# Residual rows behind their chunk's tokens, and five tiles in one routing chain, in the last stage of a graph and mixture-of-experts kernel

## Chip, core and metric

The program runs on one core of one Trainium2 chip. The metric is the device time of one execution in microseconds (us). Six runs of the kernel before gave a median of 3677.98 us, from 3671.99 to 3696.28.

## What is computed

The reference is four rounds, each a graph layer and then a feed-forward layer with experts, over x of 3125 rows (nodes) by 256. Both edits lie in the last layer, which in the reference is this:

```python
mu = mean(x, -1); var = mean(square(x - mu), -1)
xn = (x - mu) * rsqrt(var + EPS) * gamma + beta     # a second layer norm: x is already normed
logits = xn @ Wr + br                               # 8 experts
top_vals, top_idx = top_k(logits, 2); w = softmax(top_vals)
for e in range(8):
    h = gelu(xn @ W1[e] + b1[e])                    # 256 -> 512
    y = y + (h @ W2[e] + b2[e]) * w_full[..., e]    # 512 -> 256
x = x + y
```

## The kernel before

**Tiles and chunks.** The 3125 rows lie in 25 tiles of 128, with partition p of tile t holding row 128 t + p. The tile `XX` keeps x and its normed form beside each other. The last layer works through three chunks of tiles, `CH3` (L97): chunk 0 is tiles 0 to 4, with 208 places for each expert (2 blocks of 104); chunks 1 and 2 are tiles 5 to 14 and 15 to 24, with 384 places (3 blocks of 128).

**Routing, `route3` (L2624) and `Experts.route` (L1989).** One chain routes a group of up to five tiles. For each tile, ScalarE applies the batch norm of the graph layer (L2632), TensorE turns it back to rows (L2638) and VectorE adds it to x (L2640). Then come the statistics (L1891, L1892), two inverse square roots in small VectorE steps over the whole group (L221 to L232, twice, because of `twice=True`), the normed rows (L1911 on ScalarE or L1913 on VectorE), and for each tile a transpose (L1866), a scaled copy (L1873 or L1876) and the logits (L1928, L1930). The top two are found for the whole group in small VectorE steps (L289 to L317, with a Tanh on ScalarE, L307). Two matmuls count the places (L2013, L2014), more small steps make the positions (L2019 to L2057), and GpSimd scatters each tile's rows twice, once for each of its two experts, into the chunk's table `xg` in HBM (L2070, issued by the helper in L160). A memset of one element (`apart`, L1940) stands ahead of each scatter.

**Residual rows, `base_rows` (L2232).** Each tile of x is also scattered to the output (L2241, issued in L160 as `out_x<-XX,idI`), 25 scatters in all. The experts' results are added onto these rows later.

**Experts, `run` (L2132).** For each chunk and each of the 8 experts: SyncE loads the expert's places (L2107) and its weights (L2127, two halves, two buffers each); TensorE turns the places (L2155) and ScalarE scales them (L2160); TensorE makes the hidden layer (L2093), with a Gelu on ScalarE (L2181), and the output (L2097); VectorE adds the bias (L2204), ScalarE or VectorE multiplies by the routing weight (L2210, L2212), and GpSimd adds the rows onto the output in HBM, one indirect DMA for each block (L2247): 2 for each expert of chunk 0 and 3 in the others, 64 in all. An expert's adds wait until those of the expert before it in the same chunk have landed, and the first expert's wait for the chunk's residual rows (`add_rows`, L2251). The result `ro_y` has two buffers.

**What sets the order.** The engines work in program order, and a small planner (`Plan`, L1791) writes that order down. Each chain yields an engine, a planned duration and what it needs; the planner always takes the step that can start first, and among those within 0.05 us the one of the lowest rank. Routing chains are added with ranks 0, 1, 2 and so on (L2659), tokens, weights and residual rows with rank 0, experts with 1.5. Two routing chains are under way at a time: chain i + 2 starts when chain i has placed its scatters.

**Two runs of the planner.** The first, `pl.run(routed, ...)` (L2664), ends when every group is routed and no buffer of a ring is open. Then `rest` (L2258) asks whether any expert had more rows than places: a matmul turns the flag (L2262), VectorE reduces it (L2266), each engine loads it to a register and branches (L2268). What was not placed before is placed behind the branch by the second `pl.run()` (L2667).

The groups of the routing chains are (chunk, first tile, tiles):

```python
groups3 = ((0, 0, 3), (0, 3, 2), (1, 5, 5), (1, 10, 5), (2, 15, 5), (2, 20, 5))
```

Below, the five-tile groups at tiles 5, 10, 15 and 20 are called B, C, D and E; the two small groups of chunk 0 are a and b, and the group of tiles 0 to 4 is A. The experts are e0 to e7 of chunk 0, 1 or 2.

Of the kernel before, what the change touches and what calls it, by code (L numbers as in the profile page):

```python
# [115 lines left out]
def tile_gnn_ffn(ctx: ExitStack, tc: tile.TileContext, a: dict, out: bass.AP):  # L116
# [7 lines left out]
    @contextmanager  # L124
    def psums(**bufs):
        with tc.tile_pool(name="psum", bufs=1, space=PSUM) as p:
            before = dict(banks)
            banks["pool"], banks["bufs"] = p, bufs
            yield
            banks.update(before)  # L130

    def ps(tag, shape):
        return banks["pool"].tile(shape, F32, name=tag, tag=tag, bufs=banks["bufs"][tag])
# [11 lines left out]
    def bcast(src, n, pool, name):  # L145

        t = pool.tile([P, n], F32, name=name)
        nc.sync.dma_start(t, bass.AP(tensor=src.tensor, offset=src.offset, ap=[[0, P], [1, n]]))
        return t
# [9 lines left out]
    def put(table, idx, src):  # L159
        return nc.gpsimd.indirect_dma_start(  # L160
            out=table, out_offset=bass.IndirectOffsetOnAxis(ap=idx, axis=0), in_=src, in_offset=None)
# [106 lines left out]
    def load_w(pool, w, name):  # L268

        k, n = w.shape  # L270
        t = pool.tile([P, k // P, n], F32, name=name)
        nc.sync.dma_start(t, w.rearrange("(k p) n -> p k n", p=P))
        return t
# [1609 lines left out]
    def norm_steps(dst, src, n, pool, pre, ready, twice=False, which=("ACT",)):  # L1883


        st = pool.tile([P, GT, 6], F32, name=pre + "st", bufs=1)
        mv = pool.tile([P, GT, 2], F32, name=pre + "mv", bufs=1)
        nm = pool.tile([P, GT], F32, name=pre + "nm", bufs=1)
        for i in range(n):
            f = yield "DVE", 0.41, (ready[i],)  # L1890
            nc.vector.bn_stats(st[:, i, :], src[:, i, :])  # L1891
            nc.vector.bn_aggr(mv[:, i, :], st[:, i, :])  # L1892
        s = {}
        f = yield from small_steps(rsq_steps(s, "r", mv[:, :n, 1], n, pool, pre, 1), f)
        r = s["r"]
        if twice:
            v2 = pool.tile([P, GT], F32, name=pre + "v2", bufs=1)
            f = yield "DVE", 0.26, (f,)
            nc.vector.tensor_mul(v2[:, :n], mv[:, :n, 1], r)
            nc.vector.tensor_mul(v2[:, :n], v2[:, :n], r)  # L1900
            f = yield from small_steps(rsq_steps(s, "r", v2[:, :n], n, pool, pre + "2", 1), f)
            f = yield "DVE", 0.08, (f,)
            nc.vector.tensor_mul(s["r"], s["r"], r)
            r = s["r"]
        f = yield "DVE", 0.08, (f,)
        stt(nm[:, :n], mv[:, :n, 0], -1.0, r, op0=OP.mult, op1=OP.mult)
        done = []
        for i in range(n):
            done.append((yield which, 0.58, (f,)))
            if plan[0].on == "ACT":  # L1910
                nc.scalar.activation(dst[:, i, :], src[:, i, :], AF.Identity, bias=nm[:, i : i + 1], scale=r[:, i : i + 1])  # L1911
            else:
                nc.vector.tensor_scalar(dst[:, i, :], src[:, i, :], r[:, i : i + 1], nm[:, i : i + 1], op0=OP.mult, op1=OP.add)  # L1913
        return done

    def logit_steps(lg, src, g, w, b, n, ready, R, pool, name, us, *args, **kw):

        last = None
        for i in range(g + 1):
            if i < g:  # L1920
                xt = pool.tile([P, 2, P], F32, name=name, bufs=2)
                xf = yield from turned_steps(R["tp"], xt, src[:, i, :], ready[i], us, *args, **kw)
            if i:
                f = yield "PE", 0.4, (last[1], R["u"])
                free = R["u"].take()
                pl_ = ps("u", [P, 2, D])[:, 0, :n]
                for k in range(2):
                    nc.tensor.matmul(pl_, last[0][:, k, :], w[:, k, :], start=(k == 0), stop=(k == 1))  # L1928
                f = yield "DVE", 0.08, (f + slack[0],)
                nc.vector.tensor_add(lg[:, i - 1, :], pl_, b)  # L1930
                free.t = f
            last = (xt, xf)
        return f
# [3 lines left out]
    def apart():  # L1937


        nc.gpsimd.memset(gap, 0.0)  # L1940

    class Experts:
# [289 lines left out]
        def base_rows(self):  # L2232

            for c, (t0, t1, _, _) in enumerate(self.chunks):
                for t in range(t0, t1):
                    while self.x_in[t].t is None:
                        yield None, 0.0, (self.x_in[t],)
                    h = NV if t == NT - 1 else P
                    f = yield "POOL", 1.4, (self.x_in[t],)
                    apart()  # L2240
                    st = put(self.table, idI[:h, t : t + 1], X[:h, t, :])  # L2241
                    self.in_order(st, [])
                    self.bases[c].append(st.ins)
                    self.based[c].add(f)
# [296 lines left out]
    with tc.tile_pool(name="w3", bufs=1) as wp:  # L2541
# [3 lines left out]
        def halves(name, k):  # L2545
            t = wp.tile([P, 2], F32, name=name)
            nc.sync.dma_start(t, a[k].rearrange("(k p) -> p k", p=P))
            return t
# [64 lines left out]
        with tc.tile_pool(name="f3", bufs=1) as fp, psums(tp=2, mm=2, y=2, u=2):  # L2613
            g3, b3 = halves("f_ga", "L3_ffn_gamma"), halves("f_be", "L3_ffn_beta")
            rw = load_w(fp, a["L3_ffn_Wr"], "f_rw")
            br = bcast(a["L3_ffn_br"], 8, fp, "f_br")
            ex3 = Experts("L3_ffn", 8, AF.Gelu, CH3, fp, xg3, None, g3, b3, out)

            pl = plan[0] = Plan()
            R = {"tp": Ring(2), "mm": Ring(2), "y": Ring(2), "u": Ring(2)}  # L2620
            groups3 = ((0, 0, 3), (0, 3, 2), (1, 5, 5), (1, 10, 5), (2, 15, 5), (2, 20, 5))
            routed, befores = All(len(groups3)), [At(0.0), At(0.0)]

            def route3(c, t0, g, pre, before, after):  # L2624
                yield None, 0.0, (before,)
                s = slice(t0, t0 + g)
                ready = []
                for t in range(t0, t0 + g):
                    yn = fp.tile([P, 2, P], F32, name=pre + "yn", bufs=2)
                    f = yield "ACT", 0.85, ()  # L2630
                    for k in range(2):
                        nc.scalar.activation(yn[:, k, :], Y[:, k, t * P : (t + 1) * P], AF.Identity,  # L2632
                                             bias=be[:, k : k + 1], scale=ga[:, k : k + 1])
                    f = yield "PE", 0.3, (f, R["u"])
                    free = R["u"].take()
                    pt = ps("u", [P, 2, D])[:, 0, :]
                    for k in range(2):
                        nc.tensor.transpose(pt[:, k * P : (k + 1) * P], yn[:, k, :], ident)  # L2638
                    f = yield "DVE", 0.33, (f,)
                    nc.vector.tensor_add(X[:, t, :], X[:, t, :], pt)  # L2640
                    free.t = ex3.x_in[t].t = f
                    ready.append(f)
                ready = yield from norm_steps(XN[:, s, :], X[:, s, :], g, fp, pre + "n", ready, twice=True,
                                              which=("ACT", "DVE"))
                lg = fp.tile([P, GT, 8], F32, name=pre + "lg")
                f = yield from logit_steps(lg[:, :g], XN[:, s, :], g, rw, br, 8, ready, R, fp, pre + "xt", 0.42, g3, b3,
                                           which=("ACT", "DVE"))
                yield from ex3.route(c, t0, g, lg[:, :g], f, X, R, pre)
                after.t = f
                routed.add(f)  # L2650

            def experts3():
                for c in range(3):
                    yield from ex3.run(c, R)

            with tc.manual_schedule(engines={EN.PE, EN.DVE, EN.Activation, EN.Pool, EN.SP}):
                for i, q in enumerate(groups3):
                    befores.append(At())
                    pl.add(i, route3(*q, f"f{i % 2}_", befores[i], befores[i + 2]))  # L2659
                pl.add(0, ex3.tokens())  # L2660
                pl.add(0, ex3.weights())
                pl.add(0, ex3.base_rows())
                pl.add(1.5, experts3())
                pl.run(routed, R.values())  # L2664
                ex3.rest(range(NT))
                pl.meet(6.0)
                pl.run()  # L2667
# [64 lines left out]
```

## Time and profile before

| what | value |
|---|---|
| median of the six runs | 3677.98 us |
| profiled execution | 3683.83 us |
| its span (what the views cover) | 3682.1 us |
| TensorE, share of the span busy | 61% |
| VectorE, GpSimd, ScalarE | 46%, 46%, 26% |
| granted TensorE clock, mean | 0.763 |

All times of the trace are from the start of the span. "PE" is TensorE's matmul row and "PEld" its weight load, DVE is VectorE, ACT ScalarE, POOL GpSimd, SP SyncE. A line of a timeline has the start, the duration, the engine, the line of the kernel, the instruction, output <- inputs, shapes and the count of instructions merged into it; in brackets stands how long the engine was idle before and what ended that. TensorE does a float32 matmul in two instructions, so counts in the trace are twice those in the code. The table of windows has for each stretch the busy time of every engine with its instructions in parentheses, then the granted clock (1.00 is full), the DMA engines' mean busy share and GB/s.

The last layer's routing begins at about 3312 us, and the span ends at 3682.1; the edits can reach only these 370 us.

### The profile page before, as it was taken

What the parts mean: (1) busy time and instruction counts of PE and PEld (TensorE: products, weight loads), DVE (VectorE), ACT (ScalarE), POOL (GpSimd) and SP (SyncE); (2) the same over time, 40 slices, a digit from 0 to 9 for tenths busy, and PEclk for the clock granted to TensorE, in tenths of its full rate; (3) what the DMA queues carried; (4) which work ended last, traced back from release to release, by engine and by line L of the source; (5) the groups of instructions that cost most, each with busy time, mean ns of one, the idle gap of its engine ahead of it and who ended that gap; (6) DMA issues with size and microseconds to landing.
All of it is one profiled execution on the core that took longest, in us unless ns stands there. A gap on an engine that the chain in (4) does not pass through costs nothing. (4 is left out here: it accounts for less than half of the span.)

```text
span 3682.1 us, 35829 instructions
## 1 busy us (share of the span) xinstructions
PE 2243.0 (61%) x10124; PEld 1535.4 (42%) x10124; DVE 1684.8 (46%) x6003; ACT 941.8 (26%) x2072; POOL 1694.5 (46%) x1976
## 2 busy tenths in 40 slices
PE   6999667688887796692213664566621021225798
PEld 2444334355554475572102453455510021124676
DVE  3554335555657675333555345246743143336511
ACT  3555232233333342220001221122300000013333
POOL 2200254354545510415665454444457576654744
PEclk8999778689988898795555785778855555555899
DMA  8999776467776530604322563556423233323665
GB/s 293 366 373 352 240 234 190 123 219 226 245 222 180 169 97 34 251 35 156 86 82 83 172 197 113 161 177 212 154 75 106 80 96 89 90 91 102 163 156 119
DMA packets 244620, 608.06 MB, mean 165 GB/s; under 512 B 47342, under 2 KB 111439, under 8 KB 231466
## 3 DMA queue, kind: packets, MB, share of 16 engines
q1 hardware_dynamic: 138346, 321.21, 26.3%
q0 software_dynamic: 103824, 282.18, 25.4%
q10 hardware_dynamic: 2224, 2.11, 0.2%
q8 instruction: 87, 1.43, 0.2%
q14 instruction: 139, 1.14, 0.1%
HBM read 395.45 MB, written 211.44 MB: 165 GB/s over the span
## 5 line engine op out<-in xcount | busy, mean ns | idle before, releaser
L156 POOL DMA_INDIRECT g<-part,e_code x392 | 375.3, 958 | 593.7 <-DMA f<-in_attr 199.0
L156 POOL DMA_INDIRECT g_rows<-tab,srcI x413 | 401.0, 971 | 274.5 <-DVE ACC L2461 117.5
L156 POOL DMA_INDIRECT g_row<-tab,srcI x413 | 396.2, 959 | 193.6 <-issue 111.8
L646 PE MATMUL t<-w_big,n_xt 128*128 128x512 f32 x800 | 359.0, 605 | 21.0 <-issue 8.7
L2093 PE MATMUL mm<-ro_xt,ro_w 128*128 128x192 f32 (+3 forms) x928 | 253.4, 428 | 74.1 <-issue 40.6
L2097 PE MATMUL y<-ro_w,ro_h 128*96 128x256 f32 (+2 forms) x1040 | 259.3, 405 | 43.5 <-issue 26.1
L2595 PE MATMUL mm<-g_xt,c_wr 128*128 128x128 f32 x200 | 48.9, 389 | 367.0 <-issue 296.0
L2585 DVE TENSOR_TENSOR ACC<-ACC,g_row 128x256 f32<-128x256 f32 x413 | 174.0, 424 | 177.0 <-DMA g_row<-tab,srcI 147.5
L2093 PEld LDWEIGHTS mm<-ro_xt,ro_w 128*128 128x128 f32 x928 | 188.3, 224 | 124.3 <-issue 58.0
L646 PEld LDWEIGHTS t<-w_big,n_xt 128*128 128x128 f32 x800 | 151.8, 194 | 206.6 <-issue 184.4
L1011 PE MATMUL w<-xt,w_big 128*128 128x256 f32 (+1 forms) x832 | 227.9, 406 | 8.2 <-issue 8.2
L2097 PEld LDWEIGHTS y<-ro_w,ro_h 128*96 128x96 f32 (+2 forms) x1040 | 189.3, 188 | 94.5 <-issue 30.3
L883 DVE TENSOR_TENSOR g<-pw,g 128x512 f32<-128x512 f32 x196 | 127.8, 687 | 198.0 <-remote 51.4
L2461 DVE SCALAR_TENSOR_TENSOR ACC<-g_rows,g_e,ACC 128x256 f32<-128x256 f32 x413 | 201.1, 487 | 25.6 <-DVE ACC L2461 5.9
L1020 PE MATMUL w<-w_big,b_h 128*128 128x256 f32 x800 | 209.6, 399 | 2.8 <-issue 2.8
L892 PE MATMUL agg<-g,s 128*32 128x256 f32 x1568 | 155.2, 450 | 76.1 <-ACT p_out L896 27.9
L2595 PEld LDWEIGHTS mm<-g_xt,c_wr 128*128 128x128 f32 x200 | 40.5, 282 | 374.8 <-issue 299.6
L1011 PEld LDWEIGHTS w<-xt,w_big 128*128 128x128 f32 x832 | 154.2, 204 | 65.9 <-issue 45.9
L1020 PEld LDWEIGHTS w<-w_big,b_h 128*128 128x128 f32 x800 | 153.7, 199 | 41.0 <-issue 16.7
L649 ACT COPY n_tst<-t 128x512 f32<-128x512 f32 x200 | 116.8, 585 | 198.8 <-PE t L646 179.0
L2181 ACT ACTIVATE ro_h<-mm,ro_w 128x192 f32<-128x192 f32 (+3 forms) x232 | 107.1, 464 | 228.4 <-PE mm L2093 109.1
L160 POOL DMA_INDIRECT xg<-XX,ro_pos x100 | 100.6, 1006 | 140.6 <-issue 78.9
(593 smaller groups left out, 4186.1 us busy)
## 6 DMA issues: line engine op xcount, KB each, us to landing
part<-n_tst SPq DMA_DIRECT2D x100, 1024.0 KB
ro_w<-in_L_ffn_blocks SPq DMA_DIRECT2D x58, 514.0 KB
ro_w<-in_L_ffn_blocks SPq DMA_DIRECT2D x58, 512.0 KB
part<-p_out SPq DMA_DIRECT2D x98, 256.0 KB
xg<-zero SPq DMA_DIRECT2D x78, 200.0 KB
f<-in_attr SPq DMA_DIRECT2D x49, 256.0 KB
b_at<-in_edge_attr SPq DMA_DIRECT2D x50, 224.0 KB
tabn<-v SPq DMA_DIRECT2D x11, 768.0 KB
```

What stands on the lines that cost most here:

```text
L156: return nc.gpsimd.indirect_dma_start(out=dst, out_offset=None, in_=table, in_offset=bass.IndirectOffsetOnAxis(ap=idx, axis=0))
L646: nc.tensor.matmul(pt.rearrange("p r d -> p (r d)"), xt_of[t][:, k, :], wrel[:, k, 2 * i : 2 * i + 2, :].rearrange("p r d -> p (r d)"), st ...
L649: nc.scalar.copy(stage[0][:, o : o + 2, 0, :], pt)
L883: nc.vector.tensor_tensor(m, biased.pop(0), m, op=OP.mult)
L892: nc.tensor.matmul(pa[32 * j : 32 * j + 32, h, :], s[:, 2 * j + h, :], rows[4 * g + 2 * (j // 2) + h][:, j % 2, i * D : (i + 1) * D], star ...
L1011: nc.tensor.matmul(ph, w["01"][:, e, k, i * P : (i + 1) * P], xt[:, k, : n * h], start=(k == 0), stop=(k == 1))
L1020: nc.tensor.matmul(py, last[:, k, i * h : (i + 1) * h], w["02"][:, e - 1, k, :], start=(k == 0), stop=(k == 1))
L2093: nc.tensor.matmul(ph, w[:, o : o + P], xt[:, k, :], start=(k == 0), stop=(k == 1))
L2097: nc.tensor.matmul(py, h[:, i, s], w[:, i * D : (i + 1) * D], start=(i == 0), stop=(i == self.fc - 1))
L2181: nc.scalar.activation(h[:, i, :], ph, self.act, bias=w1[:, j : j + 1])
L2461: stt(u, g[:, r, :D], e[:, r0 + r : r0 + r + 1], u, op0=OP.mult, op1=OP.add)
L2585: nc.vector.tensor_tensor(u, u, rows.pop(r), op=OP.max)
```

## The change

1. `base_rows` now waits until all token scatters of the chunk have been placed (`self.sent[c]`), before it places the chunk's residual rows. The rows are the same and go to the same places.
2. Tiles 0 to 4 are routed in one chain of five instead of a chain of three and a chain of two. There are five chains rather than six.

```diff
         def base_rows(self):
             for c, (t0, t1, _, _) in enumerate(self.chunks):
+                while self.sent[c].t is None:
+                    yield None, 0.0, (self.sent[c],)
                 for t in range(t0, t1):
-                    while self.x_in[t].t is None:
-                        yield None, 0.0, (self.x_in[t],)
                     h = NV if t == NT - 1 else P
-                    f = yield "POOL", 1.4, (self.x_in[t],)
+                    f = yield "POOL", 1.4, (self.x_in[t], self.sent[c])
                     apart()
                     st = put(self.table, idI[:h, t : t + 1], X[:h, t, :])
...
-            groups3 = ((0, 0, 3), (0, 3, 2), (1, 5, 5), (1, 10, 5), (2, 15, 5), (2, 20, 5))
+            groups3 = ((0, 0, 5), (1, 5, 5), (1, 10, 5), (2, 15, 5), (2, 20, 5))
```

Because a planner writes the order, the two edits move much more than they name. In the changed program's order of instructions:

- **GpSimd.** Before: 5 residual rows, 7 token scatters of chunk 0, 5 residual rows of chunk 1, the last 3 of chunk 0, and so on; ahead of the branch lie 50 token scatters, all 25 residual rows and all 16 adds of chunk 0. After: 10 token scatters of chunk 0, 2 of chunk 1, the 5 residual rows of chunk 0, 8 of chunk 1, adds of e0, 7 of chunk 1, adds of e1, 3 of chunk 1, the 10 residual rows of chunk 1, adds of e2, and then token scatters of chunk 2 and adds of e3 to e6 in turn. The 10 residual rows of chunk 2 and the 2 adds of e7 come behind the branch, ahead of the adds of chunk 1.
- **TensorE.** Before: ranks of a and b, L2638 of B, logits of B, L2638 of C, ranks of B, then e0 of chunk 0; then the logits of C, e1, the rest of D's L2638, e2, logits of D among e3's matmuls, e4, logits of E among e5's, ranks of E, e6, e7, the transposes and half the hidden layer of e0 of chunk 1, the branch. After: L2638 of A and B (ten tiles in turn), logits and ranks of A and B, L2638 of C, logits of C, then e0 with C's ranks behind its hidden layer; L2638 of D, e1, logits of D among e2's matmuls, L2638 of E and D's ranks, e3, logits of E (three of them ahead of e4's first matmul), e4, ranks of E, e5, e6, e7, the branch. Nothing of chunk 1 is ahead of the branch.
- **VectorE** issues 68 fewer instructions: the small steps of one chain. Nine tiles of L2640 stand ahead of the first statistics (four before), and B's statistics alternate with the first small steps of A. `apart` and every other helper are unchanged.

## The prediction

> **What bounds the kernel now.** The edits reach only the last 370 us, so I read the windows by stage first, then TensorE's and GpSimd's timelines at the joints, and the chain of waits last. Windows:
>
> ```profile
> 3308.00:3343.00 35.00, 13.75 (x52) 9.96 (x52) 26.23 (x192) 11.53 (x28) 6.02 (x11) 0.51 0.28 110
> 3343.00:3374.00 31.00, 12.47 (x50) 9.30 (x51) 19.78 (x90) 8.87 (x21) 20.69 (x39) 0.50 0.29 97
> 3374.00:3492.00 118.00, 96.49 (x427) 80.45 (x426) 62.48 (x345) 47.97 (x111) 80.21 (x129) 0.80 0.58 157
> 3492.00:3507.00 15.00, 9.70 (x38) 7.34 (x39) 1.56 (x6) 3.08 (x6) 4.50 (x6) 0.89 0.39 100
> 3507.00:3682.00 175.00, 164.93 (x686) 122.53 (x684) 27.83 (x74) 66.28 (x119) 80.72 (x95) 0.99 0.58 139
> ```
>
> The columns are PE, PEld, DVE, ACT, POOL, clock, DMA share, GB/s. There are three regimes: a front of small VectorE steps (3308 to 3374), chunk 0's experts with routing among them (to 3492), and, behind the branch, chunks 1 and 2, where TensorE is busy 94% at full clock.
>
> The chain of waits names GpSimd's adds (L2247) and their DMAs for the tail, which would make the residual rows matter there. The timelines say otherwise; first all engines, then GpSimd alone:
>
> ```profile
> 3535.00 5.34 PE L2097 MATMUL y<-ro_w,ro_h 128*128 128x256 f32 x24
> 3539.43 0.51 ACT L2210 ACTIVATE ro_y<-ro_y,ro_wt 128x256 f32<-128x256 f32 x1 [3.18 <-issue]
> 3540.18 5.32 PE L2093 MATMUL mm<-ro_xt,ro_w 128*128 128x384 f32 x16
> 3540.22 1.57 POOL L2247 DMA_INDIRECT out_x<-ro_y,ro_at  x1 [5.56 <-ACT ro_y L2210]
> ```
>
> ```profile
> 3495.21 1.58 POOL L160 DMA_INDIRECT xg<-XX,ro_pos  x1 [0.20 <-issue]
> 3502.91 0.10 POOL L1940 MEMSET gap<- 128x1 f32 x1 [6.12 <-DMA xg<-XX,ro_pos]
> 3507.23 1.59 POOL L2247 DMA_INDIRECT out_x<-ro_y,ro_at  x1 [4.22 <-ACT ro_y L2210]
> ```
>
> GpSimd sits idle 5.56 us before each expert's first add, for ScalarE, which waits for TensorE; TensorE's hidden layers start 11.0 us apart (3529.19, 3540.18) with no gap. So the tail is TensorE's, and the end moves with the time at which TensorE gets through chunk 0 and the branch. TensorE in chunk 0:
>
> ```profile
> 3374.14 0.93 PE L2155 MATMUL tp<-ident,ro_x 104*128 104x104 f32 x4
> 3375.34 5.68 PE L2093 MATMUL mm<-ro_xt,ro_w 128*128 128x208 f32 x16 [0.27 <-ACT ro_xt L2160]
> ...
> 3384.68 0.60 PE L1866 MATMUL tp<-ident,XX 128*128 128x128 f32 x4
> ...
> 3392.32 1.04 PE L1928 MATMUL u<-f_rw,f_xt 128*128 128x8 f32 x4 [2.73 <-ACT f_xt L1873]
> ...
> 3394.39 1.73 PE L2093 MATMUL mm<-ro_xt,ro_w 128*128 128x208 f32 x4
> ...
> 3409.54 3.98 PE L2093 MATMUL mm<-ro_xt,ro_w 128*128 128x208 f32 x16
> ...
> 3470.35 5.89 PE L2093 MATMUL mm<-ro_xt,ro_w 128*128 128x208 f32 x16
> ```
>
> Here the logits of C stand between e0 and e1 from 3384.68 to 3394.39 and half idle, and the same 16 instructions take 3.98 us in e2 but 5.68 in e0 and 5.89 in e6.
>
> **The change, by TensorE's path.** Sums are made against the profiled execution (3683.83 us: span 3682.1 and 1.7 around it), 5.85 above the median of 3677.98; I take the difference over to the median.
>
> 1. *Start of e0: +3.3.* Nine tiles of L2640 now stand ahead of the first statistics, not four; in the trace they come 0.77 us apart (3313.49, 3314.27, 3315.04): +3.9. Five pairs of B's statistics (0.53 each) alternate with A's first small steps, which otherwise go 0.2 apart with both chains in the gaps: 5 x 0.43 = +2.2. Five tiles instead of three wait for one top-two pass, with B's copies between: +1.0. B's places then follow A's, as long as E's took alone from its ranks (3470.1) to its first scatter (3474.27): +4.2. So C's first L2640 goes from C standing behind B (B's own was at 3342.7) to 3342.7 + 11.3 = 3354.0. From there to a last logit a five-tile group took 3342.7 to 3366.0, 23.3 us, giving 3377.3; e0's transposes stand right behind, against 3374.14. Tokens are no bound: A's first scatter at about 3350, ten at 1.27 us, 3363 (before: 3361.0), landed and loaded well before 3377. In the 23.3 lies a stall of 4 to 5 us of VectorE and ScalarE at 3358.4 that the trace doesn't explain; without it the term is -0.7. The other end: if A and B go one behind the other, B's 30.6 us alone (3342.7 to its ranks at 3373.3) end at 3373.3, and e0 starts 23.3 later at 3396.6: +22.5. I take +3.3, the row with both chains' steps in each other's gaps being what the trace shows at 3319 to 3324.
> 2. *C's logits leave chunk 0: -10.4*, the 9.7 us from 3384.68 to 3394.39 and 0.7 for the fifth logit among e1's matmuls. They are now in the front, inside the 23.3 above.
> 3. *Clock: -3.9.* e1 ran cold after the stalls of C's logits (5.8 us for its 16 instructions against 3.8 in e2, without overlaps); after the change it stands where e2 stood, behind an expert's work without a long wait: -2.0. E's ranks held TensorE 2.44 us and left e6 cold (5.7 against 3.8): -1.9. The other end is 0 for both.
> 4. *E's ranks and logits: -1.0.* The ranks come after 8 us of e4's work instead of 6, so the wait of 2.44 goes; three logits ahead of e4's matmuls wait for copies: C's waited 1.36 and 2.73 in that position, B's not at all; I take +1.4. Ends -2.4 and +1.7.
> 5. *Half of e0 of chunk 1 moves behind the branch: 0.* It took 3486.72 to 3491.51, 4.8 us; behind the branch the same transposes, the wait for the copy (1.28) and 8 instructions. The branch itself keeps its price (3491.78 to 3497.30). VectorE's bias of e7 now stands ahead of the check: +0.4.
> 6. *GpSimd: 0.* Of the five rows of chunk 0 nothing is won: at 3314 to 3321 GpSimd had nothing else. Chunk 1's ten rows, 12.7 us, delay e2's adds by some 5 us and chunk 2's tokens, which nobody needs before 3590. Chunk 2's ten and e7's two adds (10 x 1.27 + 2 x 1.9 = 16.5) come behind the branch. GpSimd comes back 5.6 us after TensorE (3502.91, 3497.30) and is free for chunk 1 at 22.1 after it; e0's rows are ready at about 14. So it starts 8 late. Cover: each expert leaves it over 5 us idle, and both buffers of `ro_y` allow TensorE 11 us of lead. If the wait for landings took all idle time, the lateness would stay: +8. But at the chunks' last experts the adds began 10.35 us after the previous ones (3573.21, 3583.56), so 0.65 each is regained at least, 9.8 over 15 experts. SyncE's order of tokens and weights is the same but for three loads moved by one place at the branch; each is needed 10 us or more after it.
>
> Sum: 3.3 - 10.4 - 3.9 - 1.0 + 0.4 = **-11.6 us**: 3672.2 in a profile, 3666.4 as a median.
>
> [...]
>
> **Rivals.**
>
> - *A front as long as the gain.* The change is meant to send tokens first, but by term 1 tokens go out later (3363 against 3361), because ten tiles share one round. If B's copies also block A's on VectorE and ScalarE by another 10 us, e0 starts 13.3 late, and 13.3 - 14.9 = -1.6 is left: 3676. For it: VectorE was already busy 75% at 3308 to 3343 with five tiles. Against: the small steps of two chains fit in each other's latency.
> - *All of TensorE's gaps close.* Without C, chunk 0 has only D and E among its experts; if e1 to e7 run warm (8 x 7.8 us as e2 with its output, and 1.9 for a cold e0), ten tiles of D and E take 1.5 each in L2638, L1866 and L1928 (2.0 in the groups, mostly at half clock) and their waits stay at 10, it takes 89.3 us, not 112.8 (3374.1 to 3486.9): -23.5 + 3.3 + 0.4 = -19.8: 3658. For it: e7 ran so. Against: D's and E's waits for VectorE (3.0 and 2.8) left the clock at half afterwards.
> - *GpSimd's late start stays in the tail.* Its 8 us come back at the end: -4: 3674. Against it the 10.35 above.
> - *Slower: A and B in sequence.* VectorE works in program order; if one instruction of B that waits for TensorE stands ahead of A's chain round after round, C starts after B. e0 at 3396.6: +22.5 - 10.4 - 3.9 - 1.0 + 0.4 = +7.6: 3686. It decides from e0 starting later than 3374.1 + 14.9 = 3389.
>
> **How the numbers follow.** Forecast 0.60 (3666.4, own range 3659 to 3674), long front 0.15, closed gaps 0.13, late GpSimd 0.05, slower 0.07. The range takes in closed gaps and reaches near the slower case, as the runs of before themselves spread 24 us: 3655 to 3684. A difference under 0.5% (18.4 us) is about what measurement can't tell from no change: faster than 3659.6 is the closed gaps and an edge of the forecast, 0.16; slower than 3696.4 needs e0 33 us late, 0.04; within, 0.80.
>
> **What would show it.** In the profile after: e0's transposes at about 3377, with C's logits just before; A's first token scatter near 3350; e1's 16 instructions in about 4 us; TensorE at the branch near 3480 and back near 3486; ten residual rows right after it on GpSimd, idle time before adds back to about 5 us within a few experts; hidden layers still 11.0 us apart. Wrong if e0 starts after 3389, or if after the branch the hidden layers come more than 11.2 apart, waiting for `ro_y`.

## The result and the profile after

The changed kernel is slower by 0.42%: ratio 1.0042, interval 1.0031 to 1.0054 (3701.69 us median of 26 runs, 3686.43 of 52 runs of before beside them). Forecast were 11.6 us less; it became 15 more.

The windows of the changed kernel by stage, columns as above (PE, PEld, DVE, ACT, POOL, clock, DMA share, GB/s), with the borders moved to its own joints:

```profile
3308.00:3343.00 35.00, 17.95 (x69) 13.12 (x69) 25.49 (x138) 14.98 (x36) 0.00 (x0) 0.53 0.23 91
3343.00:3390.00 47.00, 14.79 (x61) 11.90 (x61) 24.57 (x147) 9.27 (x22) 26.94 (x50) 0.50 0.24 81
3390.00:3499.00 109.00, 80.49 (x383) 67.26 (x383) 51.00 (x272) 41.52 (x98) 66.16 (x105) 0.83 0.54 147
3499.00:3524.00 25.00, 16.69 (x61) 11.44 (x60) 2.71 (x11) 5.80 (x10) 14.66 (x25) 0.80 0.50 145
3524.00:3701.00 177.00, 163.95 (x676) 121.69 (x676) 27.87 (x74) 66.28 (x119) 83.93 (x99) 0.98 0.59 138
```

The front is 16 us longer (47 us in its second part against 31), though over the whole front no engine is more than 6.5 us busier (TensorE, 17.95 + 14.79 against 13.75 + 12.47; GpSimd 0.2). Chunk 0 is only 9 us shorter (109 against 118), and the joint behind the branch is 10 longer (25 against 15). So look at what TensorE waits for. At C's logits, all engines:

```profile
3371.86 0.86 PE L1928 MATMUL u<-f_rw,f_xt 128*128 128x8 f32 x4
...
3381.67 0.17 DVE L1930 TENSOR_TENSOR f_lg<-u,f_br 128x8 f32<-128x8 f32 x1 [8.60 <-remote]
...
3383.93 0.96 POOL L160 DMA_INDIRECT xg<-XX,ro_pos  x1 [0.19 <-issue]
...
3387.33 0.46 ACT L1873 ACTIVATE f_xt<-tp,f_be,f_ga 128x128 f32<-128x128 f32 x1 [14.71 <-remote]
...
3387.84 1.04 PE L1928 MATMUL u<-f_rw,f_xt 128*128 128x8 f32 x4 [12.74 <-issue]
...
3390.21 0.94 PE L2155 MATMUL tp<-ident,ro_x 104*128 104x104 f32 x4
```

Nobody works but GpSimd, and nobody waits for GpSimd. TensorE's matmuls for the second tile end at 3372.72 (3371.86 + 0.86); VectorE's add of that result begins at 3381.67, 9 us later. ScalarE's copy waits for TensorE's semaphore too, and begins at 3387.33. "Remote" and "issue" are names for a releaser that the view could not find. The trace also records the updates of each engine's semaphore: one of TensorE's stands at 3381.65 and one at 3387.25, 0.02 and 0.08 ahead of the two instructions above, though TensorE's last matmul was over at 3375.10. **TensorE's work was done; its signals came, counted from that last matmul, 6.5 and 12.1 us late.** (The ends of matmuls are modelled in the trace, so a matmul that itself ended late would look the same; the last section comes back to this.) GpSimd issued 25 scatters in a row, 1.27 apart, from 3353.46 to 3384.89. The same at D's logits:

```profile
3430.70 0.51 PE L1928 MATMUL u<-f_rw,f_xt 128*128 128x8 f32 x4
...
3437.50 0.96 POOL L160 DMA_INDIRECT out_x<-XX,idI  x1 [0.19 <-issue]
...
3442.18 0.17 DVE L1930 TENSOR_TENSOR f_lg<-u,f_br 128x8 f32<-128x8 f32 x1 [2.87 <-remote]
3442.40 1.02 PE L1928 MATMUL u<-f_rw,f_xt 128*128 128x8 f32 x4 [10.92 <-DVE f_lg L1930]
```

The row at 3437.50 is the last of chunk 1's ten residual rows, which change 1 put here. Three updates of TensorE stand at 3442.16, 3442.19 and 3442.22, 10.7 us after its last matmul: as if held back, then let go together. And behind the branch, TensorE's timeline:

```profile
3505.80 1.30 PE L2155 MATMUL tp<-ident,ro_x 128*128 128x128 f32 x5 [6.73 <-DMA xg<-XX,ro_pos]
...
3515.81 5.34 PE L2097 MATMUL y<-ro_w,ro_h 128*128 128x256 f32 x24
3520.99 2.74 PE L2093 MATMUL mm<-ro_xt,ro_w 128*128 128x384 f32 x8
3527.39 4.52 PE L2093 MATMUL mm<-ro_xt,ro_w 128*128 128x384 f32 x8 [3.65 <-ACT ro_h L2181]
3531.70 0.88 PE L2155 MATMUL tp<-ident,ro_x 128*128 128x128 f32 x6
```

ScalarE's Gelu of e1 waits for a signal 3 us late, under the end of chunk 2's ten residual rows (3510.52 to 3523.5).

The trace of before had the same thing, smaller: the "stall of 4 to 5 us that the trace doesn't explain" at 3358.4 ends with five updates of TensorE at 3363.52 to 3363.69, 40 ns apart and 3.3 to 3.5 us late, after a run of scatters that ended at 3361.05. All engines of before:

```profile
3359.54 0.67 PE L1866 MATMUL tp<-ident,XX 128*128 128x128 f32 x2
...
3360.09 0.96 POOL L160 DMA_INDIRECT xg<-XX,ro_pos  x1 [0.19 <-issue]
...
3363.55 0.17 DVE L1930 TENSOR_TENSOR f_lg<-u,f_br 128x8 f32<-128x8 f32 x1 [4.69 <-remote]
3363.65 0.80 ACT L1873 ACTIVATE f_xt<-tp,f_be,f_ga 128x128 f32<-128x128 f32 x2 [5.24 <-remote]
```

On five of the seven occasions below the unchanged kernel took 3183 to 3186 us instead of 3680 to 3726, and in the traces taken then no signal of TensorE is over 1 us late in the last stage; what sets this is not known.

### The profile page after: what moved, and what is told of

Same layout as the page of the kernel before. It is cut to its first block, busy times and chain, and to the rows that moved or that the text cites. A ratio compares the mean times of both kernels' runs of the same rounds, so it can differ in the third digit from the quotient of the medians.

```text
span 3701.2 us, 35751 instructions
## 1 busy us (share of the span) xinstructions
PE 2252.8 (61%) x10120; PEld 1540.2 (42%) x10120; DVE 1677.8 (45%) x5935; ACT 942.0 (25%) x2071; POOL 1692.9 (46%) x1976
## 4 chain that ended last, share of the span: by engine, by line
issue 18%; another core or an unknown queue 13%; PE 13%; DVE 5%; POOL 4%; DMA 3%; ACT 2%; SPq 0%; POOLq 0%; DVEq 0%; ACTq 0%
PE mm L2093 3%; PE y L2097 3%; DMA out_x<-ro_y,ro_at 2%; POOL out_x L2247 2%; PE mm L1695 1%; PE y L1705 1%; POOL g_row L156 1%; DVE ACC L2461 1%; PE u L2508 1%; PE u L1928 1%; PE tp L1866 0%; POOL xg L160 0%; PE tp L2155 0%; PE mm L2595 0%
## 5 line engine op out<-in xcount | busy, mean ns | idle before, releaser
L2093 PE MATMUL mm<-ro_xt,ro_w 128*128 128x192 f32 (+3 forms) x928 | 254.8, 430 | 68.6 <-issue 36.4
```

Of the source, the lines that this page charges most:

```text
L2093: nc.tensor.matmul(ph, w[:, o : o + P], xt[:, k, :], start=(k == 0), stop=(k == 1))
```

## The experiments

Three theories. **1**: TensorE's signals reach the others late while GpSimd issues scatters back to back, and the change makes and moves such runs. **2**: the common round of ten tiles (part 2) is what costs. **3**: an instruction fetch holds the engines.

Every kernel is compared with before on its own occasion, and it is said whether signals were late. (The update behind the branch, 5 to 10 us after the last matmul in every run, and the two at the kernel's end are left out of this.) Ratios are to before, with their 95% intervals; "e0 at 62.2" means that e0's transposes begin 62.2 us after the first L2638 of the last stage.

**Rows moved alone, one chain alone, no rows, gaps.** (Before: 3185.11; no late signals.) Edits against the changed kernel, the first: the old `groups3`; the second: the old `base_rows`; the third, which leaves the residual out of the output:

```diff
-                    f = yield "POOL", 1.4, (self.x_in[t], self.sent[c])
-                    apart()
-                    st = put(self.table, idI[:h, t : t + 1], X[:h, t, :])
-                    self.in_order(st, [])
-                    self.bases[c].append(st.ins)
+                    f = yield None, 0.0, (self.x_in[t], self.sent[c])
```

the fourth, in `base_rows` and, for chunk 1's tokens, in `route`:

```diff
-                    apart()
+                    for _ in range(4):
+                        apart()
```

> Part 1 alone: residual rows behind their chunk's tokens, the first five tiles still routed as three and two. Theory 1 (TensorE's signals reach the other engines late while GpSimd issues scatters back to back): C's logits stand among e0 and e1 as before, so the front is as before (e0's transposes near 3375, within 4 us), but the ten rows of chunk 1 lie across the middle of chunk 0 and the ten of chunk 2 behind the branch: one stall of TensorE of about 9 us in chunk 0 and 5 to 6 us right behind the branch, each with TensorE's signal arriving late; 10 to 15 us slower than before (ratio 1.003 to 1.004). Theory 2 (the cost is the long common round of ten tiles, part 2): no stall over 4 us in chunk 0, within 6 us of before (ratio 1.000 to 1.0015). Theory 3 (an instruction fetch holds the engines): stalls move with the number of instructions, not with GpSimd's scatters.

Measured: 0.9997 (0.9983 to 1.0011), with e0 at 51.4. Nothing of the 1.003 to 1.004.

> Part 2 alone: the first five tiles in one chain, residual rows where before had them. Theory 1: GpSimd now sends up to 30 scatters in a row behind A's ranks (ten tokens, five rows, ten tokens, five rows), and C's logits fall under them: TensorE's signal late by 10 us or more there, e0's transposes at 3388 to 3396; but neither the stall at D's logits nor that behind the branch (0 to 2 us each): within 5 us of before (ratio 0.9985 to 1.0015). Theory 2: e0 late as in the changed kernel (3390) without a late signal, and the rest as in it: 10 to 15 us slower than before.

Measured: 0.9993 (0.9983 to 1.0002), with e0 62.2 us after the first L2638, but without a stall at C's logits.

> The changed kernel without the 25 scatters of residual rows: the residual is left out of the output, and the experts' rows are added to what stands there. Theory 1: 5 scatters fewer in the burst under C's logits and 10 fewer under D's and behind the branch: the stall at C's logits 3 to 6 us shorter than 12.7 (e0 at 3384 to 3388), the one at D's (10.9) and the wait behind the branch (3.7) under 3 us: 15 to 20 us faster than the changed kernel, ratio to before 0.9985 to 1.0005. Theory 2 (the common round): e0 still near 3390, ratio 1.002 to 1.004 less the 5 us behind the branch. Theory 3: stalls of 10 us stay.

Measured: 0.9953 (0.9934 to 0.9971), more than either theory said; e0 at 62.2.

> The changed kernel in the same order, with three more of the small memsets (about 0.3 us each) ahead of each of chunk 1's token scatters and of each residual row, so that these scatters go some 2.2 us apart instead of 1.27; GpSimd has about 40 us more to do, so the total is not the question. Theory 1 (signals pass in the gaps between scatters): TensorE's signals late by under 4 us at C's and D's logits (12.1 and 10.7 in the changed kernel), e0's transposes at 3380 to 3385, in spite of a burst that ends some 13 us later. If instead any run of scatters holds the signals up to its end, however far apart they go, the stall at C's logits gets longer with the burst (15 us or more). Theory 3: stalls unchanged at 10 to 13 us.

Measured: 1.003 (1.0016 to 1.0043). Four memsets take 0.58 us in the trace of this kernel's third run (below), one took 0.11: the scatters go 1.70 us apart, 0.73 of it between them, not 2.2. With no late signal to let through, the gaps only cost.

One chain by itself costs nothing here, where theory 2 had expected 10 to 15 us. Theories 1 and 3 can't be told apart, as nothing was late; the next runs are the changed kernel itself and before.

> The changed kernel once more. In the four runs so far the kernel before took 3185 us, not 3686, and none of their traces has a signal of TensorE that arrives over 1 us late (148 such signals in the first trace of before, 156 in the changed kernel's). Theory 1 now says that what the change costs is paid in late signals: if this run has them (before near 3686), the ratio is 1.003 to 1.0055, e0's transposes 75 to 78 us after the first L2638 and a stall of 10 us at C's and D's logits; if it has none (before near 3185), no stall over 5 us at either place, e0's transposes 62 us after the first L2638 as in the two kernels with one chain and all tokens in a row, and the ratio 0.997 to 1.000. Theory 2 (the common round costs 10 us by itself) says e0 62 us after the first L2638 against some 51 in before, and 1.001 to 1.003 in either case.

> The kernel before, for a profile beside the last one on the same chip. Without late signals: e0's transposes 51 to 53 us after the first L2638 (51.4 in the run with the rows moved alone), no stall over 4 us in the front; with them 61.5 as in the first profile.

Measured (before: 3183.54; no late signals): the changed kernel 0.9984 (0.9972 to 0.9996), where theory 2 says 1.001 to 1.003: here it is *faster*, by 3 us in the medians and 5 by the ratio. e0 comes 62.2 us after the first L2638, against 57.3 in before. The 51 to 53 for before was missed: in before B's ranks stand ahead of e0, in the kernel with the rows moved alone behind it. At C's logits, all engines of the changed kernel:

```profile
2895.32 0.86 PE L1928 MATMUL u<-f_rw,f_xt 128*128 128x8 f32 x4
...
2896.16 0.96 POOL L160 DMA_INDIRECT out_x<-XX,idI  x1 [0.19 <-issue]
...
2896.44 0.15 DVE L1930 TENSOR_TENSOR f_lg<-u,f_br 128x8 f32<-128x8 f32 x1
...
2897.67 1.80 PE L1928 MATMUL u<-f_rw,f_xt 128*128 128x8 f32 x8
...
2899.32 0.94 PE L2155 MATMUL tp<-ident,ro_x 104*128 104x104 f32 x4
```

The same program, the same run of scatters 1.27 apart; but the add follows its matmuls (2896.18) after 0.26 us, not after 9, and 2.9 us later there is e0. So scatters in a row do not make a signal late on every occasion.

**Paced rows.** Edit: the rows of chunks 1 and 2 wait one by one for the adds of an expert of the chunk before; the second kernel has the old groups as well. (Before: 3183.27; no late signals.)

```diff
-                    f = yield "POOL", 1.4, (self.x_in[t], self.sent[c])
+                    behind = self.done[c - 1][i * self.n // (t1 - t0)] if c else self.sent[0]
+                    f = yield "POOL", 1.4, (self.x_in[t], behind)
```

> The changed kernel, but the residual rows of chunks 1 and 2 go one or two at a time behind the adds of each expert of the chunk before theirs, chunk 2's therefore in the tail, where GpSimd has some 5 us idle per expert; no long run of them is left. Both theories say GpSimd comes to chunk 1 sooner behind the branch (first add of chunk 1 within 20 us of TensorE's return, no row of chunk 2 ahead of it). Where before takes 3185 (no late signals): 0 to 4 us under the changed kernel, ratio to before 0.9965 to 0.9995, as the 13.6 us of the kernel without residual rows is mostly work that GpSimd no longer has. Where before takes 3686 (late signals): theory 1 says the stalls at D's logits and right behind the branch go (under 4 us each), the one at C's stays (10 to 13 us), ratio 0.998 to 1.001 against 1.0042 for the changed kernel; theory 2 says 1.002 to 1.004.

> The same paced rows with the old routing of the first five tiles as three and two. Without late signals: e0's transposes 51 to 57 us after the first L2638, C's logits back in chunk 0, ratio to before 0.998 to 1.0005, within 5 us of the paced rows with one chain. With late signals: no long run of scatters under C's logits either, ratio 0.996 to 0.999, the fastest of all.

Measured: 0.9975 (0.9962 to 0.9988), as expected, and 0.9976 (0.9964 to 0.9989), a little better; e0 at 62.2 and 51.4. Spread rows are worth a little even where signals are on time; against the changed kernel's 0.9984 the difference lies within the intervals. Then the changed kernel and the paced rows side by side, and this time with late signals (before: 3679.73):

> The changed kernel beside the paced rows in one call. Without late signals (before near 3184): ratio 0.997 to 0.9995 again, no signal of TensorE over 1 us late in the last stage but at the branch. With late signals (before near 3686): ratio 1.003 to 1.0055 and stalls of 10 us at C's and D's logits.

> The changed kernel with the rows of chunks 1 and 2 paced behind the adds, again. Without late signals: 2 to 5 us under the changed kernel of the same call, ratio 0.996 to 0.999. With late signals theory 1 expects 10 to 18 us under the changed kernel (ratio 0.998 to 1.001): the stall at C's logits stays at 10 to 13 us, those at D's logits and right behind the branch fall under 4 us.

Measured: the changed kernel 1.0042 again (1.0018 to 1.0066), the paced rows 0.9995 (0.9977 to 1.0013): 16 us between their medians. TensorE's timeline of the paced kernel, the only two idle times over 5 us from the first of C's logits to the return from the branch:

```profile
3385.40 1.04 PE L1928 MATMUL u<-f_rw,f_xt 128*128 128x8 f32 x4 [12.04 <-issue]
...
3503.15 3.42 PE L2098 MATMUL y<-ro_w,ro_h 128*128 128x256 f32 x8 [5.50 <-PEq L2269]
```

The stall at D's logits (10.92, in the changed kernel beside it 10.79) is gone with the ten rows, that right behind the branch too; the one at C's logits, whose scatters were left as they are, is still there, and a smaller one, 4.78 us, comes at e5. That is theory 1's forecast at all three places; theories 2 and 3 have no reason for it.

**Everything paced, and the single parts again.** Edit: the tokens of chunks 1 and 2 wait for adds of chunk 0 as well, five scatters to an expert. (Before: 3185.74; no late signals.)

> One chain for the first five tiles; behind it the tokens of chunks 1 and 2 go five scatters at a time behind each expert's adds of chunk 0, residual rows one or two at a time; only the ten tokens and five rows of chunk 0 go in one run. With late signals theory 1 expects the stall at C's logits under 5 us (the run of scatters ends some 3 us behind them), under 3 us at D's and behind the branch, e0's transposes 64 to 69 us after the first L2638, ratio 0.993 to 0.997: faster than both kernels. Without late signals 0.996 to 0.999, like the paced rows alone (0.9975).

> Part 1 alone, once more, hoped for where TensorE's signals come late. With late signals (before near 3680) theory 1 expects what it expected first: one stall of TensorE of about 9 us in chunk 0 where the ten rows of chunk 1 go and 4 to 6 us right behind the branch, ratio 1.002 to 1.004. If part 2 is the harmful one, 0.999 to 1.001. Without late signals 0.9983 to 1.0011 as before.

> Part 2 alone, once more. With late signals theory 1 expects the stall at C's logits of 10 to 14 us (e0's transposes 75 to 80 us after the first L2638; 61.5 in before, 76.7 in the changed kernel) but under 4 us at D's logits and right behind the branch, ratio 1.000 to 1.002. Without late signals 0.998 to 1.000 as before.

> The changed kernel with 1.2 us instead of 0.3 us between the scatters of chunk 1's tokens and of all residual rows, once more. With late signals: if they pass in the gaps, the stalls at C's and D's logits fall under 4 us (12.7 and 10.8 in the changed kernel), e0's transposes 63 to 70 us after the first L2638, ratio 0.999 to 1.003, under the changed kernel's 1.0042 in spite of about 30 us more of work for GpSimd. If only the end of a run of scatters lets them pass, the stall at C's logits grows to 15 us or more and the ratio to 1.006 or more.

Measured: all paced 0.9984 (0.997 to 0.9998), rows behind 0.9998 (0.9985 to 1.0011), one chain 0.9992 (0.9979 to 1.0005), gaps 1.0021 (1.0009 to 1.0033): for the first three what was expected without late signals. Two of them met late signals on the next occasion (before: 3726.44):

> One chain for the first five tiles, tokens and residual rows of chunks 1 and 2 paced behind the adds, once more. With late signals (before near 3680): the stall at C's logits under 5 us instead of 12 to 12.7, under 3 us at D's and behind the branch, e0's transposes 64 to 69 us after the first L2638, ratio 0.993 to 0.997. Without: 0.997 to 0.9998 as before.

> The changed kernel with 1.2 us between the scatters of chunk 1's tokens and residual rows, once more. With late signals: if they pass in the gaps, stalls under 4 us at C's and D's logits and e0's transposes 63 to 70 us after the first L2638, ratio 0.999 to 1.003; if only the end of a run lets them pass, the stall at C's logits grows to 15 us or more, ratio 1.006 or more. Without: 1.001 to 1.004 as before.

Measured: the gaps 0.9991 (0.9972 to 1.0009), against the changed kernel's 1.0042 on two other occasions; it did not run beside them on this one. All engines of that run at C's logits:

```profile
3404.31 0.96 POOL L160 DMA_INDIRECT out_x<-XX,idI  x1 [0.15 <-issue]
...
3404.59 0.86 PE L1928 MATMUL u<-f_rw,f_xt 128*128 128x8 f32 x4
...
3405.72 0.15 DVE L1930 TENSOR_TENSOR f_lg<-u,f_br 128x8 f32<-128x8 f32 x1
...
3406.01 0.96 POOL L160 DMA_INDIRECT out_x<-XX,idI  x1 [0.15 <-issue]
```

Scatters as long as before (0.96 us), as many, and the add 0.27 us behind its matmuls (3405.45). Only the pause between scatters is another: 0.73 us instead of 0.31, and with it the rate. No signal is over 1 us late from the first L2638 to e5's output, and e0 comes after 63.1 us (76.7 in the changed kernel). The late ones that are left in chunk 0 (1.4 to 2.9 us, 3492.6 to 3503.6) come at e6 and e7, under chunk 2's tokens, which got no longer pause; and ahead of the last stage, where nothing was edited, the same run is no shorter than with late signals: its first L2638 comes at 3345.49 (in before at 3312.60 with them, at 2824.20 without). So here the signals did not wait for the end of a run of scatters: at C's and D's logits they passed with 0.73 us between the scatters. The second branch of the forecast, a longer stall, is refuted.

All paced: 1.0002 (0.9985 to 1.002). The stall at C's logits is gone and e0 comes after 68.3, as expected; but signals are late in other places (5.3 us at 3510), the branch holds TensorE 9.40 us, and 0.993 to 0.997 was missed. There six tokens, two rows and two adds had come together in a row (3494.84 to 3508.67): pacing by the planner's clock did not keep runs short on the chip.

**The two cures together**, and one chain a third time. (Before: 3184.82; no late signals.) Edit: paced rows, and four memsets ahead of chunk 1's tokens and chunk 0's rows.

> The paced rows, with 1.2 us instead of 0.3 us between the scatters of chunk 1's tokens and chunk 0's residual rows, which are those under C's logits. With late signals (before near 3680 or 3726): no stall over 4 us at C's logits (12.0 with the paced rows alone), e0's transposes 63 to 66 us after the first L2638, ratio 0.995 to 0.998: faster than before and some 20 us faster than the changed kernel. Without: 0.9975 to 0.9995, up to 6 us slower than the paced rows alone for GpSimd's 22 us of gaps.

> Part 2 alone, a third time. With late signals: a stall of 10 to 14 us at C's logits under the run of scatters (e0's transposes 75 to 80 us after the first L2638), under 4 us at D's logits and right behind the branch, ratio 1.000 to 1.002. Without: 0.998 to 1.000 as twice before.

Measured: 0.9962 (0.9948 to 0.9976), the best of all, even better than expected without late signals; and 0.9989 (0.9977 to 1.0001). Neither met late signals, so what each part alone costs under them, and the best kernel's time there, stay open.

## Why the prediction was wrong

The last stage in four pieces, from one profile each: first L2638 to e0's transposes; to the branch's matmul; that matmul and TensorE's wait behind it; to the end of the last add.

| | e0 | chunk 0 | branch | behind | sum |
|---|---|---|---|---|---|
| before, no late signals | 57.3 | 103.3 | 6.3 | 181.8 | 348.8 |
| changed, no late signals | 62.2 | 89.3 | 8.4 | 187.8 | 347.6 |
| before, late signals | 61.5 | 117.4 | 5.8 | 180.8 | 365.5 |
| changed, late signals | 76.7 | 108.6 | 7.0 | 191.7 | 384.0 |
| changed with gaps, no late signals | 62.2 | 94.7 | 10.5 | 190.7 | 358.2 |
| changed with gaps, late signals | 63.1 | 103.7 | 7.0 | 187.4 | 361.2 |
| paced rows, no late signals | 62.2 | 98.7 | 5.8 | 175.3 | 341.9 |
| paced rows, late signals | 76.7 | 108.2 | 5.8 | 174.2 | 364.8 |

(With paced rows 11.5 us of e0 of chunk 1 lie ahead of the branch, in before 4.8, in the others none.) The change by itself is worth -1.2 (347.6 - 348.8), no more than what the same kernel's sum varies by (one chain alone: 345.2, 345.5 and 348.2). With late signals before takes 16.7 longer (365.5 - 348.8) and the changed kernel 36.4: +19.7. The paced rows take 22.9 longer, the gaps 3.0. Together the change makes +18.5; the two first profiles end 19.4 apart, as the second starts the stage 0.9 later, and the medians 15.

From the forecast's -11.6 to +19.4 it is 31.0 us: 11.9 in the front (+15.2 instead of +3.3), 11.3 in chunk 0 (-4.0 instead of -15.3, the half of e0 apart), 6.9 at the branch and behind it, and that 0.9. Without late signals the forecast would have been 10.4 off: 1.6, 6.1 and 2.7.

- *Step 1 failed.* "A stall of 4 to 5 us [...] that the trace doesn't explain" was carried over at its old size; it is the term that grew. In the changed kernel C's first L1866 comes 55.6 us after the first L2638 with late signals and without; from there to e0 it takes 21.1 with, 6.6 without: 14.5 of late signals, against 4.3 in the whole front of before. The counting of two chains was right to some 2 us: C's first L2640 came at 3356.8, forecast 3354.0 (the stage began 0.9 later), and without late signals e0 comes 62.2 us after the first L2638, where the step's 3377 less the stall is some 60. The bound "e0 after 3389" was passed (3390.2), but not by the mechanism of the slower rival: A and B did share a round. And the 0.04 for "slower than 3696.4" asked for an e0 33 us late; it was 16 late, and the rest came further on.
- *Steps 2 to 4 were too high.* Without late signals chunk 0 shrank by 14.0, of which 4.8 is the half of e0 moved behind the branch: -9.2 instead of -15.3. Step 2's price was itself in part late signals: its wait of 2.73 ends with updates 2.2 to 2.3 us late (3391.79 to 3391.91), and in before without late signals C's logits hold TensorE 4.2 us, not 9.7:

```profile
2891.47 0.60 PE L1866 MATMUL tp<-ident,XX 128*128 128x128 f32 x4
...
2895.68 0.95 PE L2093 MATMUL mm<-ro_xt,ro_w 128*128 128x208 f32 x4
```

D's own waits grew, too: 3.85 and 3.62 ahead of its transposes and ranks, against 2.59 and 1.29. With late signals D's stall of 10.9 took most of the rest. The 89.3 is the very figure of the rival "all of TensorE's gaps close", but that rival took it from 112.8; before without late signals has 98.5 there.
- *Step 3's sizes held in the main, its places did not:* by their rows e1's 16 instructions take 4.7 us (1.60 + 3.08) against 6.2 (1.73 + 4.51), e6's 3.2 against 5.9. But the 16 behind D's ranks take 5.7 against 4.4, and E's ranks now stand ahead of e5, whose second half waits 3.29 for ScalarE and then takes 3.14. The wait of 2.44 us ahead of e6, from which the sum took part of this term, has a slower clock behind it in the trace of before: the granted clock is 1.00 from 3459.17 and 0.50 for 6.83 us from 3469.41, at the end of that wait.
- *Step 5.* +0.4 forecast; behind the branch 5.9 more without late signals, less the 4.8 that stood before it: +1.1; the wait at the branch +2.0, forecast 0.
- *Step 6 failed where it did not look.* GpSimd's lateness was absorbed as said: add to add 11.0 again from the third expert, and without late signals no TensorE wait for `ro_y`. But the rows were costed by GpSimd's time alone; by their effect on TensorE's signals chunk 1's ten cost some 10 us at D's logits (late signals lengthen chunk 0 by 19.3, with paced rows by 9.5), and chunk 2's ten 3.9 behind the branch (191.7 - 187.8).

So the sign of the result is that of a price which the forecast knew as a stall and did not ask after. Theory 2 is right in part: one chain brings e0 some 5 us later even without late signals, and chunk 0 pays it back. Theory 3 falls: at the same count of TensorE's, VectorE's and ScalarE's instructions the stall at C's logits is 12.74 us with 0.31 us between scatters, and with 0.73 no wait of TensorE there is over 0.5 us.

## What to carry to other kernels

An idle time that the profile gives no releaser for is a term of the sum (here VectorE's 4.69 us at B's logits in before; in the changed kernel it was 8.60 at C's): look at what else ran up to its end, and ask whether the change makes more of that. That GpSimd has time did not make its runs of scatters free: under chunk 1's ten rows TensorE waited 10.92 us at D's logits, and with these rows spread the wait was gone. So try such runs away from stretches where short steps go to and fro between TensorE and the others, or spread. The same change was 0.9984 on one occasion and 1.0042 on two others; time a change of half a per cent beside the old kernel more than once.

## What was not expected of the hardware

In the last stage it was TensorE's signals that came late; VectorE's and ScalarE's were not over 1 us late there, but for the last two of the kernel. In earlier stages VectorE's were: 44 updates in the first profile, up to 9.4 us late, and none in the profile without late signals. Of these two engines only TensorE's ends are modelled, so this speaks for late signals rather than late work. Each recorded update of TensorE's semaphore, set against the end of the last signalling matmul ahead of it, over the whole kernel before (the records are not complete):

| indirect DMAs (gathers, scatters, adds) issued by GpSimd in the 10 us ahead | first profile: updates, over 1 us late | profile without late signals |
|---|---|---|
| none to 3 | 1290, 18 | 864, 2 |
| 4 or 5 | 517, 58 | 374, 2 |
| 6 or more | 822, 379 | 1720, 0 |

Instructions take the same time in both (GpSimd's indirect DMAs 993 and 995 ns in the mean, VectorE's tensor-tensor operations 360 and 360), yet the spans are 3682.1 and 3177.0. That these 505 us are late signals throughout is likely, not shown. Nor is it shown how GpSimd's scatters and the late signals hang together, by the issuing of the scatters or by the traffic that they start, or why only on some occasions: the chip numbered 12 had two without late signals and one with them. A kernel with no pause at all between scatters was not tried.
